# A loop over 31 of 32 batch tiles, with fixed copies of the input and one output buffer per piece, in a kernel of row products

## The chip, the cores and the metric

One core of a Trainium2 chip. The metric is the device time of one execution in microseconds; every execution here was at a granted clock of 1.0, and repeats of one kernel agree within about 0.1%.

Three compute-side engines do work here: DVE (the vector engine) and ACT (the scalar engine) multiply, SP issues the transfers; 16 DMA engines carry them.

## The reference

```python
r_inputs: (4096, 256) float32
dot = einsum('bi,bj->bij', inputs, inputs)
iu, ju = triu_indices(256)
return dot[:, iu, ju]              # (4096, 32896) float32
```

Each row's products of all pairs i <= j: 4.19 MB are read, 538.97 MB are written. One multiply is made per four bytes written. The profile below shows that the writing sets the time.

## The kernel before

128 rows of the batch, one per partition, make a tile; there are 32. A tile's 32,896 products per row are cut into three pieces. Each product row i of a piece is one multiply of a stretch of x by the column x[:, i], on DVE or on ACT, whichever is estimated to be free sooner. When a piece is done, SP stores it. Four output buffers rotate. All of it is written out: 96 pieces, 8,259 multiplies.

```python
xpool = ctx.enter_context(tc.tile_pool(name="x", bufs=1))
opool = ctx.enter_context(tc.tile_pool(name="o", bufs=4))
# ... four loads of x into xt[P, groups, REPEAT, d]
for g in range(groups):                                   # 32 tiles
    for c, (lo, hi) in enumerate(zip(borders, borders[1:])):   # 3 pieces
        o = opool.tile([P, slot], F32, tag="o", name=f"o_{g}_{c}")
        # ... (the very first piece is stored in four parts)
        for row, i, j, at, length in runs(d, a, b):
            shares.multiply(                              # DVE or ACT
                o[:, at - lo : at - lo + length],
                xt[:, g, row, j : j + length],
                xt[:, g, row, i : i + 1], length)
        nc.sync.dma_start(x_out[g][:, a:b], o[:, a - lo : b - lo])
```

Of the kernel before, what the change touches and what calls it, by code (L numbers as in the profile page):

```python
# [1 line left out]

# [4 lines left out]

F32 = mybir.dt.float32
AF = mybir.ActivationFunctionType
ALU = mybir.AluOpType  # L10

P = 128
UNIT = 64


def even_borders(lo: int, hi: int, pieces: int) -> list[int]:
    units = (hi - lo) // UNIT
    return [lo + units * c // pieces * UNIT for c in range(pieces)] + [hi]


def runs(d: int, lo: int, hi: int):


    width = d * (d + 1) // 2
    for row in range(lo // width, (hi + width - 1) // width):
        at = row * width
        for i in range(d):
            a, b = max(at, lo), min(at + d - i, hi)
            if a < b:
                yield row, i, i + a - at, a, b - a  # L30
            at += d - i


class Shares:


    def __init__(self, nc):
        self.nc = nc
        self.vector = self.scalar = 0.0

    def even(self):
        self.vector = self.scalar = 0.0

    def multiply(self, dst, src, factor, length: int):
        v = self.vector + 130 + 0.51 * length
        s = self.scalar + 187 + 0.83 * length
        if v <= s:
            self.vector = v
            self.nc.vector.tensor_scalar(dst, src, factor, None, ALU.mult)  # L49
        else:  # L50
            self.scalar = s
            self.nc.scalar.activation(dst, src, AF.Copy, scale=factor)  # L52


REPEAT = 1
PIECES = 3
FIRST = [1024, 3072, 7168]


@with_exitstack  # L60
def kernel(
    ctx: ExitStack, tc: tile.TileContext, x: bass.AP, out: bass.AP
):




    nc = tc.nc
    n, d = x.shape
    width = out.shape[1]  # L70
    assert n % (P * REPEAT) == 0 and width == d * (d + 1) // 2
    groups = n // (P * REPEAT)
    total = REPEAT * width
    assert total % UNIT == 0
    borders = even_borders(0, total, PIECES)
    slot = max(b - a for a, b in zip(borders, borders[1:]))

    xpool = ctx.enter_context(tc.tile_pool(name="x", bufs=1))
    opool = ctx.enter_context(tc.tile_pool(name="o", bufs=4))

    x_in = x.rearrange("(g p r) d -> p g r d", p=P, r=REPEAT)
    x_out = out.rearrange("(g p r) c -> g p (r c)", p=P, r=REPEAT)

    xt = xpool.tile([P, groups, REPEAT, d], F32, name="x")
    cuts = sorted({0, 1, groups // 8, groups // 2, groups})
    for a, b in zip(cuts, cuts[1:]):
        if a < b:
            nc.sync.dma_start(xt[:, a:b], x_in[:, a:b])

    shares = Shares(nc)  # L90
    for g in range(groups):
        for c, (lo, hi) in enumerate(zip(borders, borders[1:])):
            o = opool.tile([P, slot], F32, tag="o", name=f"o_{g}_{c}")
            cuts = [lo, *FIRST, hi] if g == c == 0 else [lo, hi]
            for a, b in zip(cuts, cuts[1:]):
                shares.even()
                for row, i, j, at, length in runs(d, a, b):
                    shares.multiply(
                        o[:, at - lo : at - lo + length],
                        xt[:, g, row, j : j + length],  # L100
                        xt[:, g, row, i : i + 1],
                        length,
                    )
                nc.sync.dma_start(x_out[g][:, a:b], o[:, a - lo : b - lo])  # L104


# [1 line left out]
_INS = ["r_inputs"]  # L108
_OUTS = [((4096, 32896), "float32")]


# [20 lines left out]
```

## Time and profile before

| what | value | how to read it |
|---|---|---|
| time, span of the profile | 1289.94 us, 1288.1 us | the span lacks 1.85 us of the time |
| DVE, ACT busy | 76%, 75% | neither is the bound |
| data queue, share of 16 DMA engines' span | 98.1% | a mean over 16 engines |
| instruction-fetch packets | 69 | 8,192 bytes each; 57 of them lie between 180 and 1250 us |
| last landings of the last store | 1264.0 us for thirteen engines, then 1271.2, 1278.9, 1287.2 | read from the records of the sixteen parts of each store |

Three DMA engines, called Z, Y and X in the prediction, end 7, 15 and 23 us after the other thirteen, which are called the crowd below. A store lands in sixteen parts, one for each DMA engine, and the trace has the time of each part; no view of `prof` lists these times, so they were read from the trace file itself. The lines that carry all this stand in the prediction. Two more, of the transfers (piece size, median from issue to landing in us), show how deep the queue of stores is with four buffers: a store takes 12.9 us, so one that lands 43.9 us after its issue had more than two others ahead of it.

```profile
out_dram<-o SPq DMA_DIRECT2D x63, 5472.0 KB, 43.9
out_dram<-o SPq DMA_DIRECT2D x32, 5504.0 KB, 38.2
```

### The profile page before, as it was taken

Reading aid. Unit: us, or ns where it says so; the run is one execution under the profiler, and the core shown is the slowest. Engines: PE = TensorE matmul, PEld = TensorE weight load, DVE = VectorE, ACT = ScalarE, POOL = GpSimd, SP = SyncE. Lnnn points to the kernel's source line nnn. Section 1 sums busy time; section 2 is a strip of 40 time slices with the busy share of each in tenths; the row PEclk is TensorE's granted clock in tenths of the full one; section 3 lists DMA queues with packets and bytes.
Section 4 is the critical chain, followed back from the end, with each engine's and each line's share of the span. In section 5 each row is a group of like instructions: output and inputs, shape, how many; then the busy total and the mean of one; then the engine's idle time right before and its main releaser. Section 6 shows DMA issues by size and latency. Waiting matters only on the chain.

```text
span 1288.1 us, 8696 instructions
## 1 busy us (share of the span) xinstructions
DVE 978.5 (76%) x4961; ACT 964.5 (75%) x3299; POOL 0.2 (0%) x4
## 2 busy tenths in 40 slices
DVE  9997787777878778787778877787777878778760
ACT  9987787777878678787778877787777868777760
POOL 0000000000000000000000000000000000000000
DMA  9999999999999999999999999999999999999992
GB/s 375 430 433 436 436 434 434 435 432 429 429 432 432 433 436 435 433 435 432 420 433 435 434 435 429 423 434 436 432 432 432 423 435 421 431 432 419 416 433 127
DMA packets 18485, 543.73 MB, mean 422 GB/s; under 512 B 1648, under 2 KB 5744, under 8 KB 5872
## 3 DMA queue, kind: packets, MB, share of 16 engines
q1 hardware_dynamic: 18416, 543.17, 98.1%
q14 instruction: 69, 0.57, 0.1%
HBM read 4.19 MB, written 538.97 MB: 422 GB/s over the span
## 4 chain that ended last, share of the span: by engine, by line
DMA 68%; DVE 28%; issue 0%; DVEq 0%; SPq 0%
DMA out_dram<-o 68%; DVE o L49 28%; DMA x<-in_r_inputs_dram 0%; DVEq L49 0%; SPq L104 0%; DVEq L128 0%
## 5 line engine op out<-in xcount | busy, mean ns | idle before, releaser
L49 DVE TENSOR_SCALAR o<-x 128x256 f32<-128x256 f32 (+62 forms) x4961 | 978.5, 290 | 271.2 <-DMA out_dram<-o 268.3
L52 ACT ACTIVATE o<-x 128x255 f32<-128x255 f32 (+62 forms) x3298 | 963.2, 386 | 284.4 <-DMA out_dram<-o 283.6
L52 ACT ACT_TABLE_LOAD x1 | 1.3, 1283 | 0.7 <-PEq L119 0.7
L119 POOL MEMSET const-bfloat16-1.0<- 128x1 bf16 x1 | 0.1, 101 | 0.0
L119 POOL MEMSET const-uint8-127<- 128x1 uint8 x1 | 0.1, 101 | 0.0
L119 POOL MEMSET const-float32-0.0<- 128x1 f32 x1 | 0.1, 98 | 0.2 <-issue 0.2
L119 POOL MEMSET const-float32-1.0<- 128x1 f32 x1 | 0.1, 98 | 0.0
## 6 DMA issues: line engine op xcount, KB each, us to landing
out_dram<-o SPq DMA_DIRECT2D x63, 5472.0 KB, 43.9
out_dram<-o SPq DMA_DIRECT2D x32, 5504.0 KB, 38.2
x<-in_r_inputs_dram SPq DMA_DIRECT2D x1, 2048.0 KB, 13.0
out_dram<-o SPq DMA_DIRECT2D x1, 2048.0 KB, 14.3
out_dram<-o SPq DMA_DIRECT2D x1, 1888.0 KB, 18.2
x<-in_r_inputs_dram SPq DMA_DIRECT2D x1, 1536.0 KB, 7.6
out_dram<-o SPq DMA_DIRECT2D x1, 1024.0 KB, 9.9
out_dram<-o SPq DMA_DIRECT2D x1, 512.0 KB, 13.0
```

The source lines that it names most:

```text
L49: self.nc.vector.tensor_scalar(dst, src, factor, None, ALU.mult)
L52: self.nc.scalar.activation(dst, src, AF.Copy, scale=factor)
L119: nc = _bacc.Bacc("TRN2", target_bir_lowering=False, num_devices=1)
```

## The change

Its intent: with one loop body in place of 31 written-out tiles, the fetches that disturb the DMA engines (69 packets, 0.74 us for each that falls on X) should go. That a loop does away with them was an estimate; no run had shown a loop yet. The body must not depend on the tile's number except in a few addresses, so each engine first copies its tile of x to a fixed place (xv for DVE, xa for ACT), and each of the three pieces has a buffer of its own. The core of the diff:

```diff
-    def multiply(self, dst, src, factor, length: int):
+    def multiply(self, dst, x_of, j: int, i: int, length: int):
     # ... DVE takes x_of[0], ACT x_of[1]
-    opool = ctx.enter_context(tc.tile_pool(name="o", bufs=4))
+    opool = ctx.enter_context(tc.tile_pool(name="o", bufs=1))
-    cuts = sorted({0, 1, groups // 8, groups // 2, groups})
+    cuts = [0, 1, groups // 2, groups]
-    for g in range(groups):
+    def batch_tile(x_of, g, first: list[int]):
         for c, (lo, hi) in enumerate(zip(borders, borders[1:])):
-            o = opool.tile([P, slot], F32, tag="o", name=f"o_{g}_{c}")
+            o = opool.tile([P, hi - lo], F32, tag=f"o{c}", name=f"o{c}")
     # ... same multiplies, same stores, into disjoint views of out
+    batch_tile([xt[:, 0], xt[:, 0]], 0, FIRST)
+    with tc.For_i(1, groups, 1, hint_engines=[],
+        head_align_engines=[mybir.EngineType.DVE, mybir.EngineType.Activation],
+        iteration_sync="reg_based") as g:
+        now = xt[:, bass.ds(g, 1)].rearrange("p o d -> p (o d)")
+        xv = xpool.tile([P, d], F32, name="xv")
+        nc.vector.tensor_copy(xv, now)
+        xa = xpool.tile([P, d], F32, name="xa")
+        nc.scalar.activation(xa, now, AF.Copy)
+        batch_tile([xv, xa], g, [])
```

More of the change, by code (lines that the diff above doesn't have):

```diff
@@ L5 @@
 from concourse import mybir
+from concourse.ap import dram_disjoint_views
 from concourse._compat import with_exitstack
@@ L48, in multiply @@
             self.vector = v
-            self.nc.vector.tensor_scalar(dst, src, factor, None, ALU.mult)
+            x = x_of[0]
+            self.nc.vector.tensor_scalar(
+                dst, x[:, j : j + length], x[:, i : i + 1], None, ALU.mult
+            )
         else:
             self.scalar = s
-            self.nc.scalar.activation(dst, src, AF.Copy, scale=factor)
-REPEAT = 1
+            x = x_of[1]
+            self.nc.scalar.activation(
+                dst, x[:, j : j + length], AF.Copy, scale=x[:, i : i + 1]
+            )
 PIECES = 3
@@ L70 @@
     width = out.shape[1]
-    assert n % (P * REPEAT) == 0 and width == d * (d + 1) // 2
-    groups = n // (P * REPEAT)
-    total = REPEAT * width
-    assert total % UNIT == 0
-    borders = even_borders(0, total, PIECES)
-    slot = max(b - a for a, b in zip(borders, borders[1:]))
-    xpool = ctx.enter_context(tc.tile_pool(name="x", bufs=1))
-    opool = ctx.enter_context(tc.tile_pool(name="o", bufs=4))
-    x_in = x.rearrange("(g p r) d -> p g r d", p=P, r=REPEAT)
-    x_out = out.rearrange("(g p r) c -> g p (r c)", p=P, r=REPEAT)
@@ L84 @@
-    xt = xpool.tile([P, groups, REPEAT, d], F32, name="x")
-    cuts = sorted({0, 1, groups // 8, groups // 2, groups})
+    assert n % P == 0 and width == d * (d + 1) // 2 and width % UNIT == 0
+    groups = n // P
+    borders = even_borders(0, width, PIECES)
+    xpool = ctx.enter_context(tc.tile_pool(name="x", bufs=1))
+    opool = ctx.enter_context(tc.tile_pool(name="o", bufs=1))
+    x_in = x.rearrange("(g p) d -> p g d", p=P)
+    x_out = [
+        v.rearrange("(g p) c -> g p c", p=P) for v in dram_disjoint_views(out, PIECES)
+    ]
@@ L86 @@
+    xt = xpool.tile([P, groups, d], F32, name="x")
+    cuts = [0, 1, groups // 2, groups]
     for a, b in zip(cuts, cuts[1:]):
-        if a < b:
-            nc.sync.dma_start(xt[:, a:b], x_in[:, a:b])
+        nc.sync.dma_start(xt[:, a:b], x_in[:, a:b])
     shares = Shares(nc)
-    for g in range(groups):
+    def batch_tile(x_of, g, first: list[int]):
         for c, (lo, hi) in enumerate(zip(borders, borders[1:])):
-            o = opool.tile([P, slot], F32, tag="o", name=f"o_{g}_{c}")
-            cuts = [lo, *FIRST, hi] if g == c == 0 else [lo, hi]
+            o = opool.tile([P, hi - lo], F32, tag=f"o{c}", name=f"o{c}")
+            cuts = [lo, *(first if c == 0 else []), hi]
@@ L95 @@
             for a, b in zip(cuts, cuts[1:]):
                 shares.even()
-                for row, i, j, at, length in runs(d, a, b):
-                    shares.multiply(
-                        o[:, at - lo : at - lo + length],
-                        xt[:, g, row, j : j + length],
-                        xt[:, g, row, i : i + 1],
-                        length,
-                    )
-                nc.sync.dma_start(x_out[g][:, a:b], o[:, a - lo : b - lo])
+                for _, i, j, at, length in runs(d, a, b):
+                    shares.multiply(o[:, at - lo : at - lo + length], x_of, j, i, length)
@@ new lines, in batch_tile @@
+                dest = x_out[c][bass.ds(g, 1), :, a:b].rearrange("o p c -> p (o c)")
+                nc.sync.dma_start(dest, o[:, a - lo : b - lo])
+    batch_tile([xt[:, 0], xt[:, 0]], 0, FIRST)
+    with tc.For_i(
+        1,
+        groups,
+        1,
+        hint_engines=[],
+        head_align_engines=[mybir.EngineType.DVE, mybir.EngineType.Activation],
+        iteration_sync="reg_based",
+    ) as g:
+        now = xt[:, bass.ds(g, 1)].rearrange("p o d -> p (o d)")
[4 more added lines that the diff above has]
+        batch_tile([xv, xa], g, [])
```

## The prediction

> **What bounds the kernel now.** I read the page first, then the chain of waits, then the stretches of the tail, then the packet records themselves. From the page:
>
> ```profile
> span 1288.1 us, 8696 instructions
> DVE 978.5 (76%) x4961; ACT 964.5 (75%) x3299; POOL 0.2 (0%) x4
> ...
> q1 hardware_dynamic: 18416, 543.17, 98.1%
> q14 instruction: 69, 0.57, 0.1%
> ...
> DMA 68%; DVE 28%; issue 0%; DVEq 0%; SPq 0%
> ```
>
> The two compute engines are idle a quarter of the time, and the transfers of the data queue fill 98.1% of 16 engines' span. So this is a kernel bound by its DMA engines. 98.1% looks like a floor, but a mean over 16 engines can hide one that finishes late. The table of who waited for whom says the same of the compute side: it waits for buffers, that is, for stores to land, in pieces of about 4.5 us, 59 times.
>
> ```profile
> ACT o L52 <- DMA out_dram<-o: 283.6, 59, 5.4
> DVE o L49 <- DMA out_dram<-o: 268.3, 59, 5.3
> ```
>
> The stretches of the end are the telling view (columns: stretch, its length, busy time of DVE, ACT and POOL, clock, DMA share, GB/s):
>
> ```profile
> 1225.00:1250.00 25.00, 20.21 (x113) 20.11 (x77) 0.00 (x0) 1.00 0.98 421
> 1250.00:1264.00 14.00, 0.00 (x0) 0.00 (x0) 0.00 (x0) 1.00 0.95 406
> 1264.00:1272.00 8.00, 0.00 (x0) 0.00 (x0) 0.00 (x0) 1.00 0.18 77
> 1272.00:1280.00 8.00, 0.00 (x0) 0.00 (x0) 0.00 (x0) 1.00 0.10 45
> 1280.00:1288.00 8.00, 0.00 (x0) 0.00 (x0) 0.00 (x0) 1.00 0.05 22
> ```
>
> In the last 24 us a share of 0.18, 0.10 and 0.05 of 16 engines is 2.9, 1.6 and 0.8 engines: thirteen are done at 1264 us, and three go on, ending one after another. The kernel ends with its slowest DMA engine, 23 us after the crowd.
>
> Which engines, and why, the packet records tell. Every store is one row of 43,776 bytes (44,032 in the third piece) per partition, eight rows per DMA engine, 1.618 us a row (1.627 in the third piece), and the sixteen landings of each store can be told apart. In the last store they lie at 0 to 0.17 us for thirteen engines, then at 7.2, 14.9 and 23.2 us. I call the three Z, Y and X. Following each from store to store:
> - X takes 12.9 us for its eight rows like the rest, except where an 8,192-byte packet of the instruction queue falls on it: then the store takes 13.65 to 13.73 us. The packet itself takes 0.309 us, and the row beside it 2.05 us in place of 1.62. That is 0.74 us per fetch. Between 180 and 1250 us I count 34 of the 57 such packets on X.
> - Z has 18 of them, at about 0.48 us each.
> - Y has about 3. Its rows are stretched by themselves, to 1.64 to 1.66 us, and only while DVE and ACT execute; with both idle they are back at 1.62. The stretch is about 2.5 ns per instruction executed.
>
> So 69 packets, or 0.1% in the queue table, are on the critical path: they sit mostly on one engine, and the last engine sets the end. By 1090 us X is about 24 us behind. A buffer comes free only when X has finished, so from there the thirteen starve too: each third store takes them 13.6 us, and they lose some 6.5 us by the end.
>
> [...]
>
> **The change, part by part.**
> - Instruction stream. In the built streams DVE falls from 4963 rows to 321 and ACT from about 3300 to 219. The loop's body with its semaphore waits has about 170 instructions on DVE and 118 on ACT, [...] On X, 34 fetches between 180 and 1250 us and in proportion some 6 more, 40 x 0.74 = 30 us, go; X would end at 1287 - 30 = 1257 us. As a check, the thirteen without their starvation end at 1264.0 - 6.5 = 1257.5 us. They agree.
> - Copies. One 128x256 multiply took 0.36 us on DVE and a 128x255 one 0.49 us on ACT; a copy of a tile should cost the same, with the loop's branch and register work perhaps 1 to 2 us an iteration (my guess). 31 of them are up to 60 us of engine time, all in the idle time: 268 us of it on DVE.
> - Three buffers for four. A store takes 12.94 us, and DVE needs 8.46, 8.45 and 14.9 us for the pieces (the chain of waits). With three buffers, when one is freed, two stores of 25.9 us are still queued. The third piece, the longest, is ready after 14.9 + about 1.5 us, so 9 us are to spare; the first one follows late but has 12 us. The slowest engine is never starved; the others may be once they are over 9 us ahead, which costs nothing.
> - Loads. Three instead of four, the same 4.19 MB, in the same queue ahead of the stores: nothing. The registers and addresses for the three stores of an iteration are on SP, which waits 1203 us for DVE: nothing.
> - The three buffers also make fewer stores in flight: issue to landing should fall from 43.9 us to about 26 to 31.
>
> **The rivals.**
> 1. Y takes X's place. Y ended at 1278.9 us (1264.0 + 14.9), for a reason that the loop doesn't touch, since the number of executed instructions is the same. Then the span is 1278.9 + 0.9 (the gap from the last landing to the span's end now), less up to 2 us for Y's own few fetches, and the time is 1.85 us more than the span, as now: 1280 to 1282 us, 0.7% faster. For it: Y's rows are stretched in every store. Against it: a stretch that goes with executed instructions [...] might not be there when the kernel is only timed.
> 2. Y is absent from the timed runs. Then 1257.5 + 0.9 + 1.85 = 1260 us; two to four fetches left at the start, 0.74 us each, [...] make it 1261 to 1265: 2% faster, on the border.
> 3. The back-edge fetches again. If each of 31 iterations brings a block to both engines, that is 62 blocks, [...] X would gain 62 x 0.74 = 46 us on 1257: about 1305 us. [...]
> 4. A loop that drains its stores at each turn would cost 31 times some 10 to 25 us. The built stream speaks against it: the first DVE instruction of a turn waits for its own engine only, and each piece for the store of its own buffer.
>
> **Range and chances.** Rival 1 has about half, rival 2 some 37%, rival 3 and the unforeseen 13%: 0.5 x 1281 + 0.37 x 1262 + 0.13 x 1303 = 1277 us. 1259 to 1288 us should hold it 8 times in 10. Faster by over 2% needs less than about 1264.4 us, which only rival 2 gives, and not always: 0.26. Within 2%: 0.71. Slower by over 2%: 0.03.
>
> **What would show it.** The instruction queue should have some 10 packets in place of 69. The tail should lose its last step: either one engine alone is late by some 15 us (Y: a share of 0.06 after the crowd has ended), or none. DVE and ACT should wait about as long as now. If the instruction queue has 60 packets or more, rival 3 holds. If the compute engines hardly wait for stores and the DMA share falls in the middle of the run, the three buffers or the loop's turn starve the queue, and my 9 us to spare were wrong. If X still trails with no fetches on it, the whole reading falls.

## More of the kernel before

The experiments ran in batches on four chips (the record numbers them 7, 9, 14 and 2), and each batch timed the kernel before as well.

"Before" took 1289.94 us in the run that the prediction saw, and between 1289.87 and 1290.04 us as the median of each batch, so that a difference of some microseconds between batches is not one of chips.

## The result, and the profile after

The kernel after took 1292.83 us (1292.69 to 1292.96, 4 runs) beside 1289.95 us of the kernel before: 0.2% slower, ratio 1.0022 with a 95% interval of 1.0005 to 1.0039. The class is "same" at 2%, but the time is 5 us above the range that the prediction gave.

From the page of the kernel after:

```profile
span 1290.7 us, 9881 instructions
DVE 990.8 (77%) x4992; ACT 981.0 (76%) x3330; POOL 0.2 (0%) x4
...
q1 hardware_dynamic: 18400, 543.17, 98.0%
q14 instruction: 5, 0.04, 0.0%
...
L124 ACT ACTIVATE xa<-x 128x256 f32 x31 | 12.9, 416 | 3.4
L122 DVE COPY xv<-x 128x256 f32 x31 | 9.1, 294 | 4.0
...
out_dram<-o SPq DMA_DIRECT2D x63, 5472.0 KB, 30.1
out_dram<-o SPq DMA_DIRECT2D x32, 5504.0 KB, 24.7
```

The fetches went, from 69 packets to 5. The copies cost 9.1 and 12.9 us of engine time in all, beside waits that are over twenty times as long. The queue of stores is one store shallower. And the data queue is as full as before, yet the kernel isn't faster. The table of who waited for whom says that the compute side still has slack, as before (us in total, times, longest):

```profile
ACT o L58 <- DMA out_dram<-o: 272.4, 62, 4.9
DVE o L52 <- DMA out_dram<-o: 259.7, 62, 4.8
```

The stretches at the end of the kernel after (same columns as in the prediction; the share of 16 engines is the last column but one):

```profile
1264.00:1272.00 8.00, 0.75 (x6) 0.75 (x4) 0.00 (x0) 1.00 0.83 358
1272.00:1279.00 7.00, 0.00 (x0) 0.00 (x0) 0.00 (x0) 1.00 0.95 409
1279.00:1289.00 10.00, 0.00 (x0) 0.00 (x0) 0.00 (x0) 1.00 0.05 22
```

Fifteen engines are busy until 1279 us, and one works on alone for ten microseconds: 0.05 of 16 is 0.8 of an engine. The staircase of three late engines has become one step. The trace doesn't name the engines; this one is Y by its marks: its lateness grows evenly, without the steps that a fetch packet makes (the last of the five packets comes at 65 us), and its rows are longer only while DVE and ACT execute. Its eight rows of a store take 13.2 to 13.4 us where the crowd's take 12.9 to 13.0.

So X and Z lost their lateness, as predicted, and Y, which should have ended at 1278.9 us, ended at 1289.1 us. The measure that I use from here on is how much Y falls behind per tile. It comes from the sixteen landings of each store, sorted: the distance from the first landing to Y's, between two stores nine apart (three tiles), in the first third of the run, where no buffer holds back the crowd yet.

| kernel | fetch packets | semaphore updates in the trace | Y falls behind per tile, us | last landing: first engine, Y, X | time, us |
|---|---|---|---|---|---|
| before | 69 | 2,167 | 0.63 | 1264.0, 1278.9, 1287.2 | 1289.95 |
| after | 5 | 10,049 | 1.01 | 1279.1, 1289.1, with the crowd | 1292.83 |

For example, Y of the kernel after was 4.11 us behind at 170 us and 7.14 us at 286 us: 3.03 us in three tiles. From about 450 us on it stays 10.4 to 11.2 us behind, because with three buffers nobody can be further ahead: the crowd waits for Y at each tile. That is why fifteen engines end 15 us later than thirteen did before, and it costs nothing by itself, since Y is never idle. Its tiles take 39.83 us each, early in the run and late, which is the crowd's undisturbed 38.83 (12.92 + 12.92 + 12.99) plus its own 1.00.

The third column is the find that led the later experiments. The trace records updates of semaphores, the counters that one engine adds to and another waits for. In the written-out kernel only the last multiply of an engine's piece tells the others that it is done: 503 updates are not on the semaphores of transfers. In the loop, the framework gives each multiply an update of its own: 4,839 on DVE's semaphore and 3,227 on ACT's. The trace has 314 waits for these two, so nobody waits for most of the updates. Counted without the semaphores of transfers, the loop has 8,392 updates. The source doesn't show this, and neither engine's row on the page gets longer by it.

### The profile page after: what moved, and what is told of

Its sections match the earlier page's. It is cut to its first block, busy times and chain, and to the rows that moved or that the text cites. A ratio compares the mean times of both kernels' runs of the same rounds, so it can differ in the third digit from the quotient of the medians.

```text
span 1290.7 us, 9881 instructions
## 1 busy us (share of the span) xinstructions
DVE 990.8 (77%) x4992; ACT 981.0 (76%) x3330; POOL 0.2 (0%) x4
## 4 chain that ended last, share of the span: by engine, by line
DMA 59%; DVE 38%; issue 0%; DVEq 0%; SPq 0%
DMA out_dram<-o 59%; DVE o L52 38%; DMA x<-in_r_inputs_dram 0%; DVEq L52 0%; SPq L108 0%; DVEq L112 0%; DVEq L149 0%; DVEq L122 0%
## 5 line engine op out<-in xcount | busy, mean ns | idle before, releaser
L52 DVE TENSOR_SCALAR o<-xv 128x256 f32<-128x256 f32 (+63 forms) x4805 | 951.2, 281 | 267.1 <-DMA out_dram<-o 259.7
L58 ACT ACTIVATE o<-xa 128x255 f32<-128x255 f32 (+63 forms) x3193 | 936.6, 386 | 278.6 <-DMA out_dram<-o 272.4
L52 DVE TENSOR_SCALAR o<-x 128x150 f32<-128x150 f32 (+50 forms) x156 | 30.6, 279 | 3.0 <-DMA x<-in_r_inputs_dram 3.0
L58 ACT ACTIVATE o<-x 128x255 f32<-128x255 f32 (+52 forms) x105 | 30.4, 385 | 0.9 <-DMA x<-in_r_inputs_dram 0.9
L124 ACT ACTIVATE xa<-x 128x256 f32 x31 | 12.9, 416 | 3.4
L122 DVE COPY xv<-x 128x256 f32 x31 | 9.1, 294 | 4.0
L58 ACT ACT_TABLE_LOAD x1 | 1.3, 1283 | 0.7 <-PEq L140 0.7
## 6 DMA issues: line engine op xcount, KB each, us to landing
out_dram<-o SPq DMA_DIRECT2D x63, 5472.0 KB, 30.1
```

What stands on the lines that cost most here:

```text
L52: self.nc.vector.tensor_scalar(dst, x[:, j : j + length], x[:, i : i + 1], None, ALU.mult)
L58: self.nc.scalar.activation(dst, x[:, j : j + length], AF.Copy, scale=x[:, i : i + 1])
L122: nc.vector.tensor_copy(xv, now)
L124: nc.scalar.activation(xa, now, AF.Copy)
```

## The experiments

### e1: the change without its loop

The kernel after with the loop written out; the copies and the three buffers stay.

```diff
-    with tc.For_i(1, groups, 1, ...) as g:
+    for g in range(1, groups):
```

> The changed kernel with its loop written out 31 times: copies of the input and three buffers stay, the loop goes. All theories: the instruction queue has some 69 packets again, the engine they sit on is late again, 1289 to 1293 us. What tells them apart is the stretch of the rows of the engine that is late while DVE and ACT execute (18 ns a row in the kernel before, 40 ns in the changed one). Theory L, the loop raises it: about 18 ns here. Theory C, the fixed copies or the three buffers raise it: about 40 ns here.

Measured: 1289.97 us, ratio to before 1.0000 (0.9983 to 1.0017). From its page, and its last stretch:

```profile
q14 instruction: 68, 0.56, 0.1%
```

```profile
1278.00:1286.00 8.00, 0.00 (x0) 0.00 (x0) 0.00 (x0) 1.00 0.06 28
```

The fetches are back and so is X, alone at the end, with a last landing at 1286.9 us. Y ends at 1278.3 us and falls behind 0.65 us per tile, as in the kernel before. So the copies, the three buffers and the three loads together change neither the time nor Y. Both effects, the lost fetches and the slower Y, come with the loop as the framework builds it. That is theory L; its figures in ns per row are taken up under r1.

### e2: half as many multiplies

Its output is wrong, which doesn't matter for the time. Each multiply makes two product rows' worth of elements from a doubled copy, so the bytes stay and the instructions halve.

```diff
+                if pairs:
+                    rows = [(0, two[0][1], 0, two[0][3], sum(r[4] for r in two))
+                            for two in (rows[k : k + 2] for k in range(0, len(rows), 2))]
-        nc.vector.tensor_copy(xv, now)
+        for half in range(2):
+            nc.vector.tensor_copy(xv[:, half * d : (half + 1) * d], now)
```

> The changed kernel, but in the loop every two products are made by one instruction of twice the length (wrong results on purpose), so half as many instructions for the same bytes stored. If one DMA engine is slowed by the count of executed instructions: its stretch falls from 40 to about 20 ns a row, 768 rows x 20 ns = 15 us less, 1275 to 1279 us. Rival, it is slowed by the bytes or the busy time of DVE and ACT, or by the stores themselves: no change, 1290 to 1294 us.

Measured: 1490.81 us, 15.6% slower. The experiment is spoilt. Its table of waits:

```profile
ACT o L58 <- DMA out_dram<-o: 774.6, 31, 25.1
DVE o L52 <- DMA out_dram<-o: 749.6, 92, 10.3
```

ACT waits 31 times up to 25 us, once a tile, instead of 62 times up to 4.9. The scheduler had moved one ACT multiply of the third piece, which needs only the first half of the copy, to the head of the tile; so ACT waited for the third buffer before it worked on the first two, and the store queue ran dry. Nothing about Y can be read from its time. A change in the operands can change the order of work, and the waits are the place to see that.

### e3: forty small multiplies more

The kernel after with 40 one-column multiplies per tile on DVE, in time in which it waits anyway.

```diff
+                if c == 1 and x_of[0] is not x_of[1]:
+                    for k in range(40):
+                        nc.vector.tensor_scalar(
+                            idle[:, k : k + 1], x_of[0][:, k : k + 1], 1.0, None, ALU.mult)
```

> The changed kernel with 40 one-column DVE instructions more in each turn of the loop, placed where DVE waits for a store anyway. By count of instructions: 1240 more at 3 to 4 ns each on the late engine, 4 to 5 us more, about 1297 us. Rival, by busy time or bytes: under 1 us more, 1292 to 1294 us. If the turn itself were too long for the buffers, the other engines would show gaps and the late one too.

Measured: 1297.15 us, ratio to before 1.0055 (1.0039 to 1.0072), so 4.3 us more than the kernel after. The group on its page:

```profile
L110 DVE TENSOR_SCALAR idle<-xv 128x1 f32<-128x1 f32 x1240 | 77.6, 141 | 0.0
```

The 77.6 us of DVE time fit into its waits (189.7 us for stores are left of 259.7). Y falls behind 1.15 us per tile in place of 1.01, and its last landing is at 1294.1 us, 5.0 us later. The time is the 1297 us that the expectation gives for a price by the count of instructions. One column is 512 bytes in all, so it is hardly what the instructions write but that they are there: 0.14 us over 40 is 3.5 ns for a small multiply with its update (4.0 ns by the last landing; the profiled run was 0.4 us slower than the median). Whether the multiply or the update costs it, this run can't say.

### e4: the kernel before again

No edit. It shows how well the lateness of single DMA engines repeats on another run.

> The kernel before once more, to see whether the lateness of its three DMA engines (23, 15 and 7 us at the last store) and the 18 ns stretch are the same in another load of the program. All theories: 1290 us; if the stretch differs from load to load on its own, 18 ns becomes something else here and neither the loop nor the copies need be its cause.

Measured: 1289.82 us, ratio 0.9999. Last landings 1263.9, 1271.3, 1279.1 and 1287.1 us: each of the four steps repeats within 0.2 us.

### r1: a loop with one update per piece

To take the updates away and keep the loop, I wrote the kernel by hand, with semaphores of its own in place of the framework's. The body, with the parts that matter:

```python
for e in (V, A):                                   # DVE, ACT
    for sem, value in waits(e):                    # x copied; this piece's last store landed
        engines[e].wait_ge(sem, value)
    for k, (i, j, at, length) in enumerate(work[e]):
        made = ...                                 # the same multiply as in the kernel after
        if k == len(work[e]) - 1:
            made.then_inc(done[e], 1)              # SP waits for this before the store
        elif EVERY:                                # False here
            made.then_inc(count[e], 1)             # nobody waits for this
```

> The kernel after, written again by hand with its own semaphores: the same loop, the same copies, three buffers and stores, but in each piece only the last multiply of each engine adds to a semaphore (6 a turn), where the changed kernel's trace has one update for each of the 259 multiplies of a turn. Theory U (each executed instruction and each semaphore update costs the late DMA engine the same 1.75 ns): about 12 events a row, so its rows stretch by 18 to 21 ns and it ends at 1277 to 1281 us instead of 1289; time 1279 to 1283 us, 1% below the changed kernel and 0.7% below the kernel before. Rival R (running in a loop as such, by registers or jumps, makes the stretch): it stays at 38 to 42 ns a row, time 1290 to 1294 us. Instruction packets about 5 to 12 under both.

Measured: 1280.30 us (1280.20 to 1280.66, 5 runs), ratio to before 0.9926 (0.9912 to 0.9939), correct. Its page and its last stretches:

```profile
span 1278.9 us, 9294 instructions
...
q14 instruction: 5, 0.04, 0.0%
```

```profile
1262.00:1269.00 7.00, 0.00 (x0) 0.00 (x0) 0.00 (x0) 1.00 0.95 409
1269.00:1278.00 9.00, 0.00 (x0) 0.00 (x0) 0.00 (x0) 1.00 0.06 24
```

The same picture as in the kernel after, one engine alone for ten microseconds, but all of it ten microseconds earlier. Y's last landing is at 1278.8 us, as in the kernel before. Y falls behind 0.68 us per tile. This is the fastest version, 9.6 us below before and 12.5 us below after. The expected time (1279 to 1283 us) holds. The expected stretch of a row does not: 0.68 us over 24 rows is 28 ns, not 18 to 21. The figures in the expectations came from following single rows, of which only some could be followed; the landings have them all, and by the same measure the kernel before has 26 ns and the kernel after 42 ns. So an update does not cost the same as an instruction, as theory U had it. The next three runs give each its own price.

### r2: the same loop with an update on every multiply

```diff
-EVERY = False
+EVERY = True
```

> As r1_loop_one_mark, but every multiply adds to a semaphore that nobody waits on (its last one of a piece to the one that the store waits for). Theory U: back to 38 to 42 ns of stretch a row and 1290 to 1294 us, as the changed kernel. Rival R: no difference from r1_loop_one_mark, whatever that took. Rival S (the rewriting by hand, not the updates, is what made the difference): it stays at r1's time.

Measured: 1289.75 us, ratio to before 0.9998 (0.9983 to 1.0013). The last stretch:

```profile
1278.00:1288.00 10.00, 0.00 (x0) 0.00 (x0) 0.00 (x0) 1.00 0.06 26
```

The trace has 10,224 updates where that of r1 has 2,167, and the same 9,294 instructions. Y's last landing moves from 1278.8 to 1288.6 us: 9.8 us over 8,057 updates are 1.22 ns each. Y falls behind 0.97 us per tile. So rival R fails, and rival S too: the same hand-written loop is slow again once the updates are back. The time is a quarter of a microsecond below what was expected, because I had taken the kernel after's figure. In the profiled run of the kernel after 3.6 us pass from the last landing to the end of the time (1292.69 less 1289.10), in that of r2 1.4 us (1290.01 less 1288.63), as in r1 and r3. The difference of 2.2 us lies after the last landing and is put down here to the end that the framework gives a program; no run takes that end away by itself.

### r3 and r4: written out, with one update per piece, and with one on every multiply

The hand-written kernel once more, without a loop.

```diff
-LOOP = True
+LOOP = False
```

> As r1_loop_one_mark, but written out without a loop: about 69 instruction packets come back. Theory U: stretch 18 to 21 ns a row, the engine that carries most of the instruction packets is late by 20 to 25 us, the time is the kernel before's, 1288 to 1292 us. Rival R expects the same here, as there is no loop; it is the base for r4_line_every_mark.

> As r3_line_one_mark (no loop), but every multiply adds to a semaphore that nobody waits on. Theory U: without any loop the stretched engine's rows go from about 20 to 38 to 42 ns and it ends near 1289 us, next to the engine that is late by instruction packets; time 1289 to 1294 us. Rival R (a loop is needed): stretch stays at 18 to 21 ns.

Measured: 1287.51 us (ratio 0.9981) with one update per piece and 1288.89 us (ratio 0.9991) with one on every multiply. Both lie a little below the ranges expected, by 0.5 and 0.1 us. The fetches are 66 packets in both. Last stretches of the two, in this order:

```profile
1277.00:1285.00 8.00, 0.00 (x0) 0.00 (x0) 0.00 (x0) 1.00 0.06 28
```

```profile
1278.00:1286.00 8.00, 0.00 (x0) 0.00 (x0) 0.00 (x0) 1.00 0.11 50
```

0.06 is one engine at work alone, 0.11 is two. In the first it is X: last landings Y 1277.8, X 1286.0 us. In the second Y has come up to X: X 1286.2, Y 1287.6 us. The 8,062 more updates cost Y 9.9 us, 1.22 ns each, the same price as in the loop; and X moved by 0.2 us only. In this pair the two late engines are independent, and the time follows whichever is later, which is why 9.9 us on Y are only 1.4 us on the clock here. With that, the rival that a loop as such slows Y has fallen.

These two and r1 also give the worth of the change's intent when the updates don't come with it: 1287.51 to 1280.30 us, 7.2 us. With 164 instructions on DVE and 112 on ACT a turn (r1's trace), 5 fetch packets were left in the whole run of the loop, where the written-out form has 66.

### r5 and r6: small multiplies without and with an update

r1 with 42 one-column multiplies per tile on DVE, 14 ahead of each piece; first without updates, then with one on each.

```diff
+            for k in range(14 * c, 14 * c + 14):
+                small = nc.vector.tensor_scalar(
+                    tiny[:, k : k + 1], fixed[V][:, k : k + 1], 2.0, None, ALU.mult)
+                if TINY_COUNTS:                      # False in the first, True in the second
+                    small.then_inc(count[V], 1)
```

> r1_loop_one_mark with 42 one-column multiplies more a turn on DVE (14 ahead of each piece, 1,302 in all), which add to no semaphore. Theory U with the update measured by r1 to r4 (1.2 ns each) leaves for an instruction itself between 1.4 ns (the kernel before: 14.9 us late less 2,167 updates of 1.2 ns, over 8,696 instructions) and 2.8 ns (the 40 tiny ones in the loop of the changed kernel, 5.0 us over 1,240, less 1.2): the late engine ends 1.8 to 3.6 us later than in r1, time 1282 to 1284 us. Rival V (only updates cost, the instructions do not): no change from r1, 1280.3 us within 0.4. Rival W (DVE, 92% busy, now holds the stores back): the other fifteen engines no longer wait for the late one and all end together.

> r5_42_tiny_silent, but each of the 42 adds to a semaphore that nobody waits on. Theory U: 1,302 updates of 1.2 ns, 1.6 us later than r5. Rival V: 4 to 5 us later than r5, as the same number of counted tiny ones cost in the changed kernel's loop.

Measured: 1283.48 us and 1285.08 us (ratios 0.9950 and 0.9962). Y's last landing is at 1281.8 and 1283.4 us, against 1278.8 in r1. The group in the first of the two, and DVE's waits there:

```profile
L120 DVE TENSOR_SCALAR tiny<-xv 128x1 f32<-128x1 f32 x1302 | 87.2, 147 | 1.1
DVE o L83 <- DMA out_dram<-o: 179.2, 61, 3.9
```

So 1,302 instructions cost 3.0 us, 2.3 ns each (2.4 by the times), and 1,300 updates 1.6 us, 1.22 ns each. Together that is the 3.5 ns of the small multiplies in the kernel after. Rival V, under which instructions without updates cost nothing, fails: 3.2 us more than r1. Rival W fails too: Y still ends ten microseconds after the first engine, so it is not DVE that holds the stores back, and DVE still waits 179 us for them.

### r7 and r8: instructions of an engine that has no part in the work

r1 with 1,302 one-column memsets on POOL, without updates, in one go from about 265 us on.

```diff
+    nc.gpsimd.wait_ge(stored[0], 160)
+    for k in range(1302):
+        nc.gpsimd.memset(small[:, k : k + 1], 0.0)
```

> r1_loop_one_mark with 1,302 one-column memsets on POOL, an engine with no part in the kernel, straight after the tenth part or so of the run; they add to no semaphore and nobody waits for them. Theory U (the late DMA engine pays about 2.4 ns for every executed instruction, whichever engine executes it): its last landing comes 3.1 us later than in r1, time 1283 to 1284 us, and it gains on the others faster only in the stretch in which POOL works; some 10 more instruction packets at most 5 of which fall on it. Rival D (only work of DVE and ACT costs it, for instance by their writes): no change from r1, 1280.3 us within 0.5. Rival F (POOL's own instruction fetches make another engine late): the last landing belongs to an engine with fetches and no stretch, below 1283 us.

Measured: 1298.76 us, 18.5 us more than r1, which no theory had said. The stretches around the memsets:

```profile
260.00:300.00 40.00, 39.72 (x110) 30.04 (x103) 29.38 (x698) 1.00 0.94 405
300.00:316.00 16.00, 16.00 (x42) 14.63 (x53) 8.71 (x261) 1.00 0.93 398
316.00:350.00 34.00, 33.72 (x115) 8.93 (x27) 11.45 (x346) 1.00 0.44 188
350.00:400.00 50.00, 43.05 (x224) 41.16 (x145) 0.00 (x0) 1.00 1.01 435
```

While POOL works, DVE is busy all the time and gets through 2.75 multiplies a microsecond (110 in 40 us), where it does 4.5 afterwards (224 in 50 us) with time to spare. Its multiplies became longer (1,027.5 us in all, from 990.5), the stores ran out of work, and the DMA share fell to 0.44. The end says nothing about Y, because all engines were emptied and started level again at 349 us. Only the first 20 us of the memsets can be read: at the store that begins to land at 286.4 us Y was 5.98 us behind, against 5.02 us in r1. That is the direction that theory U expects; fetch packets of POOL may be part of it.

Spread out, 42 memsets a tile, each lot released when the third store of the tile before has landed, DVE's loss fits into its waits:

```diff
+    for turn in range(31):
+        nc.gpsimd.wait_ge(stored[2], 16 * (turn + 1))
+        for k in range(42 * turn, 42 * turn + 42):
+            nc.gpsimd.memset(small[:, k : k + 1], 0.0)
```

> As r7_pool_writes_too, whose single burst of 1,302 memsets starved the stores for some 20 us (DVE hardly worked beside it), but spread out: 42 memsets a turn, each lot released by the landing of the turn before's third store. DVE loses about 28 ns a memset by r7, 1.2 us a turn, which its waits for buffers (over 8 us a turn) hold. Theory U (2.3 to 2.4 ns for every executed instruction, whichever engine executes it): the late engine gains about 0.10 us a turn more than in r1 (0.78 in place of 0.68), its last landing comes 3.1 us later and the time is 1283 to 1284 us, as with the 42 on DVE in r5; the few fetch packets of POOL (about 10) change that by 0 to 3 us if they fall on it. Rival D (only instructions of DVE and ACT cost it): 0.68 a turn and 1280.3 us within 0.5.

Measured: 1283.71 us, ratio to before 0.9950. Y falls behind 0.78 us per tile, as expected and as with 42 small ones on DVE, and its last landing is at 1282.5 us, 3.6 us later than in r1, where 3.1 were worked out; the time is in the range expected.

```profile
L99 POOL MEMSET small<- 128x1 f32 x1302 | 44.8, 98 | 1199.4 <-DMA out_dram<-o 1199.4
```

Ten more fetch packets than in r1 came with it. They don't make the 0.78: Y's lateness grows by it evenly from 144 us on, while the steps of about 0.5 us after the packets at 217 and 337 us are on other engines. So Y pays for instructions of an engine that has nothing to do with the output, as much as for DVE's.

### All of them

e2 and r7 starved their stores and e4 repeats the kernel before, so they are left out.

| kernel | fetch packets | updates | Y behind per tile | last landing: first, Y, X | time, us |
|---|---|---|---|---|---|
| e1 loop written out | 68 | 2,216 | 0.65 | 1276.6, 1278.3, 1286.9 | 1289.97 |
| e3 40 small ones, after | 5 | 11,289 | 1.15 | 1284.0, 1294.1, – | 1297.15 |
| r1 loop, one update | 5 | 2,167 | 0.68 | 1269.0, 1278.8, – | 1280.30 |
| r2 loop, every | 5 | 10,224 | 0.97 | 1278.6, 1288.6, – | 1289.75 |
| r3 line, one update | 66 | 2,185 | 0.63 | 1276.5, 1277.8, 1286.0 | 1287.51 |
| r4 line, every | 66 | 10,247 | X and Y cross | 1277.5, 1287.6, 1286.2 | 1288.89 |
| r5 r1 + 42 silent | 5 | 2,166 | 0.78 | 1272.0, 1281.8, – | 1283.48 |
| r6 r1 + 42 counted | 5 | 3,466 | 0.83 | 1273.6, 1283.4, – | 1285.08 |
| r8 r1 + 42 on POOL | 15 | 2,169 | 0.78 | 1273.6, 1282.5, – | 1283.71 |

A tile has 258 multiplies (r1's expectation says 259) and two copies. 260 x 2.4 ns are 0.62 us, and 0.63 to 0.68 were measured where updates are few. 260 updates x 1.22 ns are another 0.32 us: 0.94, and 1.01 were measured in the kernel after. The hand-written loop lies 0.05 us above the written-out kernel in the same way. The loop has instructions of its own: the trace of r1 has 9,294 and that of r3 8,605, which is 22 a turn more, put down here to branches and register work (the trace of the kernel after has 733 such instructions, that of the kernel before none). At 2.4 ns each they would be 0.05 us, an estimate; no run varies them alone.

## Why the prediction was wrong, point by point

- **The bound.** Right. The kernel ends with its slowest DMA engine, before and after, and in each experiment that wasn't starved.
- **The fetches.** Right. "Some 10 packets in place of 69", an estimate of mine, as no trace had shown what a loop does to them: 5. No wait of DVE or ACT for a fetch shows in the kernel before; the cost shows on the DMA engine that carries the packets, 0.74 us each on X. X and Z now stay level with the crowd. Rival 3, the back-edge that fetches again, is false. So is rival 4, a loop that drains its stores at each turn: the data queue's share is 98.0%, and no wait of DVE or ACT is longer than 4.9 us.
- **Copies, three buffers, loads.** Right. The copies took 0.294 and 0.416 us, somewhat less than the 0.36 and 0.49 predicted, beside waits. The store queue is shallower (43.9 us became 30.1; 26 to 31 was said), the crowd is held at 10.4 to 11.2 us ahead of Y, where about 9 were worked out, and Y isn't starved. The tail of some 15 us under "What would show it" forgets this hold: with it Y alone can be late by some 10 us only, as it was. e1 shows that the three together change nothing.
- **Rival 2, Y absent in the timed runs.** Not so in the runs timed here, whose spans were recorded too. Y's end and the time move together in the kernels in which Y is the last: +3.0 and +3.2 us from r1 to r5, +9.8 and +9.5 from r1 to r2. This rival's 37% brought the predicted time to 1277 us, below the 1281 us of rival 1. (With the times of the profiled runs the two figures of each pair are equal.)
- **Rival 1, Y takes X's place.** This is what happened, and its size was wrong. The step of the prediction that failed reads: "Y ended at 1278.9 us (1264.0 + 14.9), for a reason that the loop doesn't touch, since the number of executed instructions is the same". The price of an instruction, 2.5 ns, was good (2.3 to 2.4 in r5). The missing term was the updates: in this framework's loop each multiply also changes a semaphore, at 1.22 ns (r1 to r2), and 7,882 more of them are 9.6 us. Y ended at 1289.1 us, 10.2 us after the predicted place. The number of executed instructions wasn't the same either: the page has 9,881 in place of 8,696, most of them the loop's own. Of the 10.2 us, 0.6 are left for them, less than 2.3 ns each would make; from r3 to r1, 689 more go with 1.1 us. The other part of the miss is at the very end: 3.6 us from the last landing to the time of the profiled run, where 0.9 + 1.85 was carried over from before. 1278.9 + 10.2 + 3.6 is that run's 1292.7 us.

The comparison of the built instruction streams had shown what each engine executes, and I set that beside the page. I didn't compare what each instruction signals, and that is what the loop changed. r1 is the prediction's rival 1 with almost no added updates: 1280.30 us, where it says 1280 to 1282. A part of that is luck, since the hand-written kernel ends 1.4 us after the last landing and not 2.75; with the sum's own end it would be 1281.6 us.

Why does one DMA engine pay for executed instructions and updates? No run shows it. Measured is the price, 2.3 to 2.4 ns for an instruction (r1 to r5) and 1.22 ns for an update (r1 to r2), and that an uninvolved engine's instructions cost as much (r8: 0.78 us per tile, as in r5). An estimate from 0.63 and 1.01 us a tile over 32 tiles is 20 us of that engine's time in the kernel before and 32 us in the kernel after. Each run here has its span recorded, so none tells whether Y is late in a run that records nothing. If it were not, the kernel after might be the faster one. That stays open.

## What to carry to other kernels

When a kernel is bound by its transfers and the mean share looks like a floor, look at the end of it engine by engine: here fetches that fill 0.1% of the DMA engines' time fell mostly on one of the sixteen, and the loop without them and without new updates was 7.2 us faster (r3 to r1); updates that no engine's row shows fell on another, and cost 9.5 us (r1 to r2). When a change replaces written-out code by a loop, compare not only the instructions but also what each of them signals. And if one late engine is cured, work out from its own terms when the next one would end, and ask of each term whether the change touches it.
